# Projecting queries and keys without padding, in a four-block sequence model whose attention alternates with other matmuls

## The chip, the cores and the metric

The kernel runs on one core of a Trainium2 chip. Everything is 32-bit floating point. The metric is the time of one execution on the device in microseconds (us). The engines are TensorE (PE, with its weight load PEld), VectorE (DVE), ScalarE (ACT), GpSimd (POOL) and SyncE (SP, which here only issues transfers). All runs of the kernel before: 2048.16, 2049.68 and 2059.28 us, median 2049.68.

## The reference

Four blocks act on x, which has 4 sequences of 512 tokens with 288 features, under one condition vector for each sequence.

```python
def attention(h):                      # blocks 0, 1 and 3; 16 heads of 18
    q, k, v = split(h @ w_qkv + b_qkv)     # block 3: no biases here
    p = softmax(q @ k.T * 18 ** -0.5)      # 512 x 512 for each head and sequence
    return (p @ v) @ w_proj + b_proj

# blocks 0, 1, 3: six vectors from the condition shift, scale and gate
x = x + gate1 * attention(layernorm(x) * (1 + scale1) + shift1)
h = layernorm(x) * (1 + scale2) + shift2
x = x + gate2 * feed(h)
# feed, block 0: top 2 of 4 experts (288 -> 1152 -> 288, gelu by tanh)
# feed, blocks 1 and 3: one MLP of the same size (gelu by tanh; exact gelu)

# block 2: U from QR of a 288 x 64 matrix, R = expm(skew matrix of the condition)
x = x + (x @ U @ R - x @ U) @ U.T
```

## The kernel before

**Stages.** L0's attention, the experts, L1's attention and MLP, the rotation of block 2, L3's attention and MLP follow one another. The QR and the matrix exponential of block 2 are done in small portions beside other stages.

**Rounds.** An attention has 16 rounds, `groups[r]`: batch b = r // 4, group g = r % 4 of four heads. A head has 18 features, padded to 32 partitions, so that a group fills the 128 partitions of a tile (`qks[r, 0]` for queries, `qks[r, 1]` for keys, three buffers each, shifting through rounds). The score work is in quads of four matmuls with 32 rows each, which run side by side in PE's four row groups: two from `row_max` (queries against keys; DVE takes the maximum of each row straight from the bank) and two from `weight` (keys against queries of an earlier round, one round and one quad behind; ScalarE takes the exponential from the bank). `shift` ends a round: four transposes bring the row maxima into a bank, and DVE subtracts them from the queries, in a nineteenth row of each head, against which the keys hold a one. Thus the second product has the maximum subtracted already. A round has eight quads; after quads 1 and 5 come `sums`, the products of the exponentials with the values.

**Gaps.** After each quad other work is put in by a dictionary `pieces` from gap number to a string, one letter for each piece: Q is `queries_and_keys` of the next round, X is values (`values`) or output projection (`project`), A transposes the next batch's activations, R is routing for the experts. The order of PE is fixed as written: `mm` (line 76) ties each matmul to the one before it, so every matmul has line 76 in the profile. `take`, `beside_of` and `in_turn` fix the order of other engines in the same way, without a wait. `work_off` takes pieces; at the round's end what remains of each job is drained.

**Banks.** PSUM has eight banks (line 64): four with the tag "sc" for the tiles of the quads, three with the tag "de" for everything else (`misc`), and one, `av`, for the sums. A tag's banks are used in turn; a tile waits until its bank's last reader is done.

**Projection.** `queries_and_keys` (lines 829 to 857) multiplies weights that lie padded in DRAM: 8 column chunks of 128, four for queries and four for keys, of which each round takes one and one. The 288 input features are two chunks of 128 and a remainder of 32. ScalarE adds the bias and writes the tile of queries or keys in place (line 856). The bias holds the one of the nineteenth row.

**After the scores.** `collect` sends the raw sums of a round by POOL's queue (`oo<-raw`, 18 x 512 each), and the sums' divisors by SP's queue; `invert` (lines 964 to 974) sends them back inverted. The queue of SP also carries all loads, and in block 0 the copies of expert weights into a table in DRAM (`w1c`).

**Start of block 0.** SP loads x of batch 0, then the attention's weights, and with `load_x` (lines 171 to 173) twelve tiles of x of batches 1 to 3. The first round's projection is made before any score (`first`), and its successors' in the gaps.

**Experts and MLP.** `contraction` (lines 1286 to 1301) multiplies the hidden features by the second weights, into "de" banks; the hidden products use "sc" banks. The rotation (`rotate`, line 1983 on) uses "de" for its small products.

## Time and profile before

The profiled execution took 2033.07 us (its span, from first to last instruction, 2031.4), 16.6 us or 0.8% less than the median of the runs above.

| stage | window, us | PE busy, us | DVE busy, us | ACT busy, us | DMA share |
|---|---|---|---|---|---|
| start | 0 to 48 | 37.28 | 23.51 | 7.51 | 0.73 |
| attention L0, rounds 1 on | 48 to 391 | 334.27 | 243.93 | 167.60 | 0.25 |
| experts | 391 to 931 | 519.08 | 208.71 | 154.07 | 0.59 |
| attention L1 | 931 to 1285 | 342.21 | 269.00 | 168.47 | 0.18 |
| MLP L1 | 1285 to 1470 | 184.19 | 73.72 | 46.52 | 0.17 |
| rotation | 1470 to 1500 | 27.21 | 11.32 | 9.56 | 0.00 |
| attention L3 | 1500 to 1847 | 338.17 | 210.45 | 167.16 | 0.12 |
| MLP L3 | 1847 to 2031 | 174.81 | 33.68 | 44.54 | 0.07 |

The windows are cut at the first and last instructions of a stage as the timeline shows them, to the nearest us. Busy time is the time in which an engine executed something; the DMA share is the mean busy share of 16 DMA engines. A line of the timeline gives the start, the duration, the engine, the line, the operation, output and inputs by name (numbers of buffers left out), then shapes, the number of instructions in the row and, in brackets, the idle time before it and what ended it. Durations of matmuls that follow one another overlap, so what one costs is read from the starts.

### The profile page before, as it was taken

To read this page: it belongs to the slowest core of one execution; us is meant where nothing else is said; L and a number is where in the kernel's file an instruction comes from. 1 tells how busy PE (TensorE), PEld (TensorE's weight loads), DVE (VectorE), ACT (ScalarE), POOL (GpSimd) and SP (SyncE) were. 2 spreads that over 40 slices of the span, in tenths; PEclk is the share of its full clock that TensorE was granted. 3 is DMA by queue.
4 is the path that set the end of the run, shared out by engine and by line. 5 is a ranking of instruction groups with operands and counts; after the bars stand their busy time and mean duration, and the time that the engine had idled before them with its cause. 6 is when DMAs were issued, how large, how long until landed. Compare 5 with 4: busy or idle time off the path is not lost.

```text
span 2031.4 us, 29536 instructions
## 1 busy us (share of the span) xinstructions
PE 1957.2 (96%) x10932; PEld 1045.6 (51%) x10932; DVE 1074.3 (53%) x3103; ACT 765.4 (38%) x1409; POOL 569.2 (28%) x803
## 2 busy tenths in 40 slices
PE   7999999999999999999999999999999999999998
PEld 4434444466667777776434443456654344433565
DVE  5666777623454333446777877454255556554211
ACT  1545555333312232322555544421125455555220
POOL 3111221443434446651332122211401111213101
PEclk9989999899999999999999999999999899999999
DMA  7421111447655766751112111220000111111000
GB/s 152 119 52 20 23 33 34 106 121 222 180 155 163 223 191 206 220 183 30 45 42 43 33 39 40 47 69 19 21 1 10 28 29 35 28 27 23 18 16 22
DMA packets 95698, 155.89 MB, mean 77 GB/s; under 512 B 33571, under 2 KB 71310, under 8 KB 95554
## 3 DMA queue, kind: packets, MB, share of 16 engines
q0 software_dynamic: 28672, 89.90, 14.7%
q1 hardware_dynamic: 66770, 64.10, 13.8%
q8 instruction: 86, 1.41, 0.3%
q14 instruction: 58, 0.48, 0.1%
q10 hardware_dynamic: 112, 0.01, 0.0%
HBM read 125.29 MB, written 18.48 MB: 71 GB/s over the span
## 4 chain that ended last, share of the span: by engine, by line
PE 70%; DVE 7%; DMA 4%; POOL 1%; issue 1%; ACT 1%; SPq 0%; POOLq 0%; DVEq 0%; ACTq 0%
PE e0h L76 9%; PE e0o L76 8%; PE a3m L76 7%; PE a1m L76 6%; PE av L76 6%; PE a3psqk L76 4%; PE f1h L76 4%; PE f3h L76 4%; PE a1psqk L76 4%; PE f1o L76 3%; DVE max L873 3%; PE f3o L76 3%; DMA v<-pT 2%; DMA wr<-in_wrot 1%; PE a3psv L76 1%; PE a3pp L76 1%
## 5 line engine op out<-in xcount | busy, mean ns | idle before, releaser
L873 DVE TENSOR_REDUCE max<-a3m 128x1 f32<-128x512 f32 x256 | 164.6, 686 | 132.9 <-PE a3s L76 122.3
L76 PE MATMUL e0h<-e0hT,e0w 128*128 128x256 f32 (+1 forms) x1188 | 229.0, 404 | 4.9 <-DMA e0w<-w1c,wrow 4.2
L873 DVE TENSOR_REDUCE max<-a0m 128x1 f32<-128x512 f32 x256 | 165.3, 683 | 94.3 <-PE a0s L76 81.7
L873 DVE TENSOR_REDUCE max<-a1m 128x1 f32<-128x512 f32 x256 | 165.8, 684 | 75.0 <-PE a1s L76 68.4
L76 PE MATMUL e0o<-e0w,e0hm 128*128 128x288 f32 x756 | 201.6, 417 | 0.0
L76 PEld LDWEIGHTS e0h<-e0hT,e0w 128*128 128x128 f32 (+1 forms) x1188 | 166.2, 189 | 62.3 <-issue 37.1
L885 ACT ACTIVATE a0p<-a0s 128x512 f32<-128x512 f32 x256 | 140.2, 596 | 146.8 <-PE a0s L76 146.7
L885 ACT ACTIVATE a1p<-a1s 128x512 f32<-128x512 f32 x256 | 140.9, 596 | 142.4 <-PE a1s L76 142.1
L885 ACT ACTIVATE a3p<-a3s 128x512 f32<-128x512 f32 x256 | 140.0, 596 | 139.2 <-PE a3s L76 139.1
L76 PE MATMUL a1m<-a1qk,a1qk 32*128 32x512 f32 x512 | 159.2, 647 | 8.0 <-DVE max L873 6.9
L76 PE MATMUL a0m<-a0qk,a0qk 32*128 32x512 f32 x512 | 159.4, 647 | 6.4 <-DVE max L873 5.3
L76 PEld LDWEIGHTS e0o<-e0w,e0hm 128*128 128x128 f32 x756 | 141.9, 192 | 42.5 <-issue 4.0
L76 PE MATMUL a0s<-a0qk,a0qk 32*128 32x512 f32 x512 | 160.4, 655 | 1.3 <-DVE max L873 1.3
L76 PE MATMUL a1s<-a1qk,a1qk 32*128 32x512 f32 x512 | 159.8, 647 | 0.2 <-DVE u L547 0.2
L76 PE MATMUL a3m<-a3qk,a3qk 32*128 32x512 f32 x512 | 152.1, 647 | 6.8 <-DVE max L873 5.5
L76 PE MATMUL a3s<-a3qk,a3qk 32*128 32x512 f32 x512 | 153.5, 647 | 0.3 <-DVE a3qk L927 0.3
L1279 ACT ACTIVATE e0hm<-e0h,e0w 128x256 f32<-128x256 f32 x189 | 89.5, 473 | 166.7 <-PE e0h L76 166.7
L607 POOL TENSOR_TENSOR nrm<-n,phalf 64x1 f32<-64x1 f32 (+31 forms) x64 | 36.6, 573 | 297.9 <-DVE n L604 294.1
L1813 ACT COPY e0r<-e0o 128x288 f32<-128x288 f32 x44 | 17.5, 398 | 184.1 <-PE e0o L76 176.4
L76 PEld LDWEIGHTS a1m<-a1qk,a1qk 32*128 32x128 f32 x512 | 47.4, 184 | 72.8 <-DVE max L873 44.1
L76 PEld LDWEIGHTS a0m<-a0qk,a0qk 32*128 32x128 f32 x512 | 47.4, 185 | 67.9 <-DVE max L873 38.8
L76 PE MATMUL f1h<-f1hT,w 128*128 128x512 f32 (+1 forms) x216 | 80.8, 614 | 0.4 <-ACT f1hT L502 0.4
(465 smaller groups left out, 3270.0 us busy)
## 6 DMA issues: line engine op xcount, KB each, us to landing
eo<-e0r SPq DMA_DIRECT2D x44, 144.0 KB
ada<-in_ada SPq DMA_DIRECT2D x18, 324.0 KB
wr<-in_wrot SPq DMA_DIRECT2D x16, 288.0 KB
g<-gates SPq DMA_DIRECT2D x24, 144.0 KB
w1c<-in_w SPq DMA_DIRECT2D x20, 144.0 KB
w<-in_w SPq DMA_DIRECT2D x6, 432.0 KB
x<-in_x SPq DMA_DIRECT2D x16, 144.0 KB
w1c<-in_w SPq DMA_DIRECT2D x8, 288.0 KB
```

Of the source, the lines that this page charges most:

```text
L76: ins = nc.tensor.matmul(*args, **kwargs).ins
L607: in_turn("POOL", nc.gpsimd.tensor_tensor(nrm, n2, phalf[0:n], ALU.pow))
L873: take("DVE", nc.vector.tensor_reduce(m[:, t, i, D : D + 1], ps, AX.X, ALU.max))
L885: take("ACT", nc.scalar.activation(p, ps, AF.Exp, scale=D**-0.5))
L1279: nc.scalar.activation(self.hms[i][f], ps[r][:, 0 : self.width], func, bias=b1(f)),
L1813: take("ACT", nc.scalar.copy(y, ps))
```

## The change

- The padded weights of queries and keys become 576 columns without padding, in five chunks of 126 columns (7 heads of 18; the last has 72). `queries_and_keys` computes one chunk in a round, two in the round before a new batch. A chunk is two remainder matmuls and four products of 256 tokens, in two "de" banks; ScalarE adds the bias into a tile `u`.
- `heads_of` sends each head's 18 rows of `u` into the padded tiles: four transfers for queries on SP's queue, issued in the round's first Q piece, from a chunk that was computed a round earlier (except in the first round and for a new batch), and four for keys issued by ScalarE, two after the chunk's last product and two in later Q pieces.
- The padding of the three sets of query and key tiles is written once (`padding`); `row_max` uses 18 rows, and `shift` multiplies the queries with a mask and subtracts the maxima in one DVE instruction.
- Banks: five "sc" and two "de". Contraction and rotation take "sc"; side work inside an attention takes "sc" (`aside_bank`).
- The strings of pieces are set anew. In odd rounds an X job that still has pieces at the round's end is left to the next round (`left`), where they are W in gap 0. A quad's order is scores, maximum, scores, maximum.
- Start of block 0: the padded weights are loaded into x's room of batches 1 to 3 (`wide`), ScalarE copies them to the compact tiles (`narrow`), then x of these batches is loaded in three transfers of 576 KB on SP's queue (`load_whole`); biases come by 11 transfers on POOL's queue. For L1 and L3 twelve transfers from DRAM to DRAM compact the weights during L0's attention (`compacting`), in runs of 72 bytes.
- The values of the first two token tiles are computed before the first scores. The routing pieces of rounds 11 to 14 move to other gaps.

```diff
-    banks = {"sc": 4, "de": 3}
+    banks = {"sc": 5, "de": 2}
...
+    def load_whole(b):
+        to = x[:, b * NT : (b + 1) * NT, :]
+        nc.sync.dma_start(to, a["x"][b].rearrange("(t p) c -> p t c", p=P))
...
+        def step(l, k, n):
+            to = compact[l][n, :, k, :]
+            src = a[f"wqk{l}"][:, k, n * NG * P : (n + 1) * NG * P]
+            src = src.rearrange("p (h e) -> p h e", e=DP)[:, :, 0:D]
+            beside_of("SP", nc.sync.dma_start(to, src))
...
             def queries_and_keys(r):
 
-                yield
                 b, g = groups[r]
...
+                early = g > 0
+                for c in range(g + 1 if g else 0, g + 2):
+                    yield
+                    if early:
+                        heads_of(r, 0)
+                    m = min(UC, 2 * C - c * UC)
+                    cols = slice(c * UC, c * UC + m)
+                    ps = [bank("de", f"{name}psqk{r}_{c}_{k}") for k in range(2)]
...
+                    for k in range(2):
+                        product(k, MC, slice(k * RR, (k + 1) * RR))
+                    u = us[b, c] = pool.tile([P, T], F32, tag="u", name=f"{name}u{r}_{c}")
+                    for k in range(2):
+                        for n in range(MC):
                             yield
...
+                            product(k, n, slice(0, P))
+                        nc.scalar.activation(
...
+                    if c == 0:
+                        heads_of(r, 0)
+
+                for i in range(GH):
+                    heads_of(r, 1, [i])
+                    if i > 0:
+                        yield
+
+            def heads_of(r, s, which=range(GH)):
+
+                b, g = groups[r]
+                for i in which:
+                    c, row = divmod((2 * g + s) * GH + i, HC)
+                    o, u = qks[r, s][i * DP : i * DP + D, :], us[b, c]
+                    if s == 0:
+                        in_turn("SP", nc.sync.dma_start(o, u[row * D : (row + 1) * D, :]))
+                    else:
+                        beside_of("ACT", nc.scalar.dma_start(o, u[row * D : (row + 1) * D, :]))
...
-                take("DVE", nc.vector.tensor_sub(q, q, ps))
+                take(
+                    "DVE",
+                    nc.vector.scalar_tensor_tensor(q, q, mask, ps, ALU.mult, ALU.subtract),
+                )
...
-                pieces = {0: "QQ", 2: "QQQ", 3: "QQQ", 4: "XQX", 6: "XX", 7: "X"}
+
+                pieces = {0: "WWQ", 2: "QQ", 3: "QQ", 4: "QXX", 5: "Q", 6: "XX", 7: "X"}
+                if g == NG - 1:
+                    pieces = {0: "QQQ", 2: "QQ", 3: "QQQ", 4: "QQ", 5: "Q", 6: "QXX", 7: "X"}
...
+                if r in left:
+                    jobs["W"] = left.pop(r)
...
-                    pieces = {0: "QQA", 2: "QQQ", 3: "QQQ", 4: "QAA", 6: "XXX", 7: "XX"}
+                    pieces = {0: "QQQ", 2: "QQ", 3: "QAA", 4: "QA", 6: "XX", 7: "X"}
...
-                    quad([(row_max, r, k)] + lagging(8 * r + k - 9))
+                    quad(lagging(8 * r + k - 9) + [(row_max, r, k)])
...
+                        if r % 2 and r < n - 1 and "X" in jobs:
+                            left[r + 1] = jobs.pop("X")
...
-                ps = bank("de", f"{self.name}o{i}_{t}")
+                ps = bank("sc", f"{self.name}o{i}_{t}")
...
-    load_x(1)
-    load_x(2)
-    load_x(3)
+    w["narrow"]()
+    for b in range(1, B):
+        load_whole(b)
```

## The prediction

> **What bounds the kernel now.** I read the page's busy row and clock row first. TensorE (PE) is the bound, at its full clock nearly throughout.
>
> ```profile
> PE 1957.2 (96%) x10932; PEld 1045.6 (51%) x10932; DVE 1074.3 (53%) x3103; ACT 765.4 (38%) x1409; POOL 569.2 (28%) x803
> PEclk9989999899999999999999999999999899999999
> ```
>
> Then the table by stage, for the rounds of the attentions of L0, L1 and L3 (columns: window, length, busy time of PE, weight load, DVE, ACT and POOL, granted clock, DMA share, GB/s). PE idles 9 to 12 us in each stage of 16 rounds, 0.5 to 0.75 us a round.
>
> ```profile
> 48.00:391.00 343.00, 334.27 (x2065) 143.72 (x2062) 243.93 (x608) 167.60 (x298) 71.11 (x113) 0.98 0.25 57
> 931.00:1285.00 354.00, 342.21 (x2032) 145.60 (x2030) 269.00 (x667) 168.47 (x295) 85.43 (x130) 0.99 0.18 39
> 1500.00:1847.00 347.00, 338.17 (x2027) 144.23 (x2026) 210.45 (x391) 167.16 (x294) 58.16 (x97) 0.98 0.12 24
> ```
>
> Last the timelines of PE, DVE and ACT inside a round of L3: they show what a gap between two quads costs when it has too little work.
>
> ```profile
> 1700.20 1.03 PE L76 MATMUL a3psqk<-a3hT,wqkr 32*128 32x512 f32 x4
> 1708.77 1.56 PE L76 MATMUL a3psqk<-a3hT,wqk 128*128 128x256 f32 x6
> 1710.27 0.69 PE L76 MATMUL a3m<-a3qk,a3qk 32*128 32x512 f32 x1
> ...
> 1563.20 1.24 PE L76 MATMUL a3psv<-wv,a3hT 128*128 128x288 f32 x4
> 1564.37 0.69 PE L76 MATMUL a3m<-a3qk,a3qk 32*128 32x512 f32 x1
> 1564.63 0.69 PE L76 MATMUL a3m<-a3qk,a3qk 32*128 32x512 f32 x1
> 1565.68 0.75 PE L76 MATMUL a3psv<-wv,a3hT 128*128 128x288 f32 x2
> 1566.27 0.92 PE L76 MATMUL a3sh<-ident,max 128*128 128x128 f32 x4
> 1567.13 0.69 PE L76 MATMUL a3m<-a3qk,a3qk 32*128 32x512 f32 x1
> ```
> ```profile
> 1563.29 1.29 DVE L873 TENSOR_REDUCE max<-a3m 128x1 f32<-128x512 f32 x2 [1.62 <-PE a3s L76]
> 1564.49 0.45 DVE L827 COPY a3v<-a3psv 128x288 f32<-128x288 f32 x1
> 1567.30 0.69 DVE L927 TENSOR_TENSOR a3qk<-a3qk,a3sh 128x512 f32<-128x512 f32 x1
> ```
> ```profile
> 1563.33 1.09 ACT L885 ACTIVATE a3p<-a3s 128x512 f32<-128x512 f32 x2 [1.83 <-PE a3s L76]
> ```
>
> The quad ends at 1563.20 (T). The pair of row maxima runs T+0.09 to T+1.38, the pair of exponentials T+0.13 to T+1.22. Two tiles of the next quad start at T+1.17, behind the gap's work; the other two need the bank of the second maximum and start at T+1.43. With four score banks, a gap with under 1.43 us of work is stretched to that.
>
> **The change, part by part.**
>
> *Projection.* Prices from L3's rows by their starts: six products of 128x256 take 1.50 us (1708.77 to 1710.27), 0.50 each; the remainder pair of 512 columns 0.96 (1700.20 to 1701.16), so 0.53 for the new pair of 256 columns, by the same rate with 0.05 of start. A batch had 4 x (0.96 + 8 x 0.50) = 19.84; it will have five chunks of 0.53 + 4 x 0.50 = 2.53, 12.65. That is 7.2 us less a batch, 86 us over 12 batches. It is a gain only where the gap it leaves has no floor.
>
> *Five banks.* The fourth tile of a quad then waits for the second exponential (T+1.22), so the floor falls to about T+1.27. An estimate from the rows above.
>
> *A plain round, worked out (L3's sixth).* A quad takes 1.06 (1562.13 to 1563.20), eight 8.5; sums of values 1.85; a product of X or W 0.58; the shift's transposes 0.62. Before, the eight gaps hold 1.46, 1.85, 1.50, 1.50, 1.66, 1.85, 1.17 and 1.20; raising the last two to 1.43 gives 12.7, with the quads 21.2 (measured from shift to shift: 21.17). After, they hold WWQ 1.69, sums 1.85, QQ 1.00, QQ 1.00, QXX 1.17, sums 1.85, XX 1.17, X and shift 1.20; raised to 1.27 that is 11.75, with the quads 20.2. So some 1.0 us of the 2.4 removed here survives the floor, before new waits. The same sum gives 20.1, 20.2, 20.3 and 20.2 for rounds 5 to 8 (measured before: 21.99, 21.17, 21.38, 21.74): 86.3 becomes 80.8.
>
> *New waits on PE in those rounds.* Two spare banks serve projection, values and shift. (i) A round that leaves X pieces has both banks full of values at its end; the shift must wait for DVE's copy (0.45), which stands behind the last quad's maxima (until T+1.38): the shift starts at T+1.83, and with its 0.62 the gap holds 2.45 in place of 1.27. Between 0 (copy done early) and 1.2; I take 1.2, since DVE runs in order. Behind the shift stands the whole next quad. (ii) The next round's Q starts with a bank whose value copy is behind two maxima: between 0 and 1.3; I take 0.7, half way, since two W products run first. (iii) ScalarE issues the keys, two and then one at a time. The only ACT issue in the trace took 0.42 (SP's take 0.4 to 0.7); the exponentials queue behind it, and the score bank behind them: 0 if in its idle time (ACT is 48% busy here), 0.84 if a pair stands in front; I take 0.4 in a plain round, and 0 in the round that projects two chunks, where the issues fall beside the long gap of the sums. In a round that also transposes the next batch, whose evacuations are ACT's too, a half-empty gap (0.53 or 1.00) and these make 0.75.
>
> With these rounds 5 to 8 come to 20.1 + 1.2 + 0.75 = 22.05, 20.2 + 0.7 + 0.4 = 21.3, 20.3 + 1.2 = 21.5 and 21.3: 86.15 against 86.3, nothing gained. Rounds 9 to 12 likewise, +0.6 in all since leftovers follow one another, and rounds 1 and 2 +0.4. Rounds 3, 4 and 13 to 15, with few pieces and no W, fall from 20.5..20.8 to the new floor: -0.7, -0.9, -1.0, -1.0 and -1.8. An attention: -4.4; three: **-13 us**. Bounds: -54 with no new wait (each attention -18: -5.5 for rounds 5 to 8, as much for 9 to 12, -5.4 for light rounds, -2 for rounds 1 and 2); +13 with (iii) at 0.84 in 13 rounds of each (13 x 0.44 x 3 = 17 more) and (ii) at 1.3 in five (5 x 0.6 x 3 = 9 more).
>
> *Start of L0.* Before, the x of batches 1 to 3 and the first scores did not touch:
>
> ```profile
> 28.26 9.03 SPq L173 DMA_DIRECT2D x<-in_x  x12
> 29.91 1.14 PE L76 MATMUL a0m<-a0qk,a0qk 32*128 32x512 f32 x8 [0.78 <-ACT a0qk L856]
> ```
>
> Now the first queries go by DMA on SP's queue, behind three x loads of 576 KB. Twelve loads took 9.03 us of issue at the DMA rate of this stretch; the queries need the data before them out of the way, then about 2 us (a 36 KB transfer SBUF to SBUF, `oo<-raw`, takes 1.9 to 2.1 to landing). First scores at 38 to 40: **+9 us**, between +3 (only key and query latency) and +13. The six narrowing copies on ACT run while the first activations are still awaited. POOL's eleven bias transfers stand before its later issues, all due tens of us later; cover gone, 11 x 0.5.
>
> *Starts of L1 and L3*: query and key DMAs in front of the first scores, 2 us, less the values moved under them: **+1.5 each, +3** (0 to 5).
>
> *Experts and rotation in the score banks.* Their outputs share the ring with the hidden products; about ten direct neighbours wait 0.4 more for a ScalarE copy (0.40 a copy): **+4** (-4, if five banks relieve it, to +10).
>
> *DVE's side work* (reflections, gates) in L0 and L1, where DVE is busy 244 and 269 us instead of 210, lengthens (i) and (ii), since the copies now gate a shared bank: **+4** (0 to +15).
>
> *Clock.* In round 4 of L0 and L3 the clock was halved for some 10 us and the round took 25.4 instead of about 20.9; the same sums row shows it.
>
> ```profile
> 1594.79 3.40 PE L76 MATMUL av<-a3p,a3v 128*19 128x512 f32 x16
> 1713.91 1.91 PE L76 MATMUL av<-a3p,a3v 128*19 128x512 f32 x16
> ```
>
> It befell rounds whose gaps are nearly empty; the change makes most rounds more like that. I take one more, **+5** (-9 if both go, +27 if six join). [...]
>
> *Compaction and the rest.* Twelve transfers of 1536 runs stand on SP's queue in L0's rounds; the nearest, 384 runs, took 0.84 to 2.3 us, so 3.4 to 9.2. What stands behind them are queries wanted a round (21 us) later and divisors wanted later still: 0, or up to +9 if one query is late each time by 0.8. The shift's subtraction becomes a three-operand form on DVE beside 0.69: 0 to +0.3 a round on the chain, counted in (i). Scores before maxima in the quad: 0, four run at once. Query transfers wait on SP for ScalarE's projection tile; behind them stand divisors and loads with rounds to spare: 0, or 9 if L0's expert loads, which fill its DMA slices, start each round 0.6 later.
>
> **Sum.** -13 + 9 + 3 + 4 + 4 + 5 = +12 us on the profiled execution's 2033.07, 2045. That execution is 16.6 us (0.8%) below the median of the runs, 2049.68; the same ratio gives **2062**. A measurement of this kernel can tell about 0.5%, 10 us, from no change.
>
> **Rivals.** *A, faster*: the waits (i) to (iii) hide, because copies slip in ahead of the maxima and key issues fall into ACT's idle half. Then -54 + 25 = -29, 2020; with the other costs at their low ends (3 + 0 - 4 + 0 - 9 = -10), 1985. For it: 86 us of work really go from an engine at 96%. Against it: DVE's order in the row at 1564.49, the copy after both maxima. It decides where less than half of the waits remains. *B, no change*: half of the waits, -33 + 25 = -8, 2041 to 2053. *C, much slower* on one mechanism: the half clock in four to ten more rounds at 4.5 us, so 2080 to 2107. For it: round 4 lost it in two attentions of three; against it: L3's last three rounds, as light, kept it.
>
> **How the numbers follow.** My forecast, slower by 0.5 to 1.5%: 0.34. C: 0.13. B: 0.19. A: 0.34. The likeliest's own range, by its bounds, is 2052 to 2080; what of it is under 2060 is counted with B. A and C both hold much, so the range runs from A's middle to C's upper part, 2000 to 2100. Faster 0.34, same 0.19, slower 0.47.
>
> **What would show it.** PE's busy time down by 80 to 90 us, and its idle time up by as much. In a plain round, the shift's first transpose more than 1 us behind the last value product, waiting for DVE's value copy; Q's remainder at gap 0 waiting for the same; exponentials behind ACT's issues. First scores of L0 at 38 us or later, released by a DMA. The half clock in more than three rounds. I am wrong if full rounds fall below 20.5 us, if the shift is not held, or if L0's scores start before 33.

## The result, and the profile after

The changed kernel takes 2166.28 us (2165.46 to 2170.8) against 2053.02 for the kernel before on the same chip: 1.055 times, 95% interval 1.052 to 1.059. The forecast was 2062, range 2000 to 2100: 0.6% slower was expected, 5.5% was measured.

The page of the changed kernel, busy row and clock row:

```profile
PE 2018.7 (93%) x10692; PEld 1058.6 (49%) x10692; DVE 1080.8 (50%) x3123; ACT 752.6 (35%) x1439; POOL 573.9 (27%) x814
PEclk9878999899996999999989899899998999999999
```

TensorE has 240 matmuls fewer and yet is busy 61 us longer than in the profile of before, where the prediction expected 80 to 90 us less; its idle time rose by 72 us, near what was expected. The longer busy time goes with a lower clock. The profile gives a mean granted clock of 0.936 against 0.983. Adding up the clock in steps of 1 us, as the window view gives it, there are 277 us at half clock (68 in the profile of before), in 33 stretches that last multiples of 3.4 us, but for the last, which the run's end shortens.

A second profile of the kernel before (2052.07 us) was taken with the experiments. It shows how far the stages vary when nothing is changed, and is the better base, since its total lies nearer the median. Stages from the first instruction of one to the first of the next, with the half clock in each:

| stage, us / half clock, us | before | before, second profile | changed |
|---|---|---|---|
| start | 30 / 0 | 29 / 0 | 34 / 0 |
| attention L0 | 380 / 24 | 376 / 17 | 410 / 85 |
| experts | 527 / 17 | 558 / 55 | 578 / 72 |
| attention L1 | 362 / 7 | 363 / 10 | 387 / 65 |
| MLP L1 | 171 / 0 | 171 / 0 | 177 / 3 |
| rotation | 38 / 7 | 34 / 0 | 37 / 0 |
| attention L3 | 354 / 10 | 349 / 0 | 370 / 44 |
| MLP L3 | 170 / 3 | 170 / 6 | 172 / 8 |

Against the second profile the span grew by 114 us: 78 in the three attentions, 20 in the experts, 5 at the start, 11 elsewhere. The experts vary by 31 us between two profiles of one kernel, so theirs is the least certain share.

In the timeline of L3 the stall that matters is in round 4. First ScalarE, then SyncE, then TensorE of the changed kernel:

```profile
1703.20 1.09 ACT L989 ACTIVATE a3p<-a3s 128x512 f32<-128x512 f32 x2 [2.02 <-PE a3m L82]
1709.19 0.74 ACTq L961 DMA_DIRECT2D a3qk<-a3u  x1
1709.98 1.57 ACT L989 ACTIVATE a3p<-a3s 128x512 f32<-128x512 f32 x3 [5.69 <-DMA a3or<-a3one]
```
```profile
1701.70 1.59 SPq L1081 DMA_DIRECT2D a3or<-a3one  x2
1703.34 8.33 SPq L193 DMA_DIRECT2D w<-in_w  x8
```
```profile
1706.35 0.33 PE L82 MATMUL a3sh<-ident,max 128*128 128x128 f32 x1 [0.42 <-DVE max L977]
1710.63 1.21 PE L82 MATMUL a3m<-a3qk,a3qk 18*128 18x512 f32 x1 [2.90 <-ACT a3p L989]
```

ScalarE finished its exponentials at 1704.3 and next had to issue one key transfer. It did so only at 1709.19, released by a transfer of SyncE's queue, the inverted divisors `a3or<-a3one`, whose data the keys don't use. The issue took 0.74 us; the wait in front of it took 4.9. Three exponentials, ready long before, stood behind it, and TensorE idled 2.90 us for their banks. L1 has the same in round 8, where ScalarE idled 9.0 us.

The trace's records also show why the issue waits. In this run all 901 transfers of SyncE and all 193 of ScalarE signal their landing on the same eight semaphores (100 and 102 to 108), and the 525 of GpSimd on eight others (111 to 118). This key transfer signals on semaphore 105. So does the transfer of the divisors that was issued at 1701.70: its last signal came at 1709.12, and ScalarE, which waited on 105, issued at 1709.19. Of the six waits of over 1 us in front of a key issue in L1 and L3, four (4.8 to 8.2 us) are of this kind, each behind a SyncE transfer of divisors. The other two, 6.6 us each in the first rounds, ended with VectorE's copy into a tile's padding (L1237). The window view cut at 3.41 us shows what follows (length, busy times of PE, PEld, DVE, ACT and POOL, granted clock, DMA share, GB/s):

```profile
1702.28:1705.70 3.42, 3.42 (x19) 1.48 (x15) 1.98 (x4) 1.09 (x2) 0.00 (x0) 1.00 0.24 20
1705.70:1709.11 3.41, 1.61 (x6) 0.43 (x3) 1.35 (x2) 0.00 (x0) 0.00 (x0) 1.00 0.30 66
1709.11:1712.52 3.41, 1.89 (x8) 1.67 (x10) 0.00 (x0) 1.57 (x3) 0.00 (x0) 0.50 0.50 135
1712.52:1715.94 3.42, 3.42 (x19) 1.78 (x18) 2.44 (x5) 1.24 (x3) 0.00 (x0) 0.50 0.17 48
1715.94:1719.35 3.41, 3.41 (x20) 0.48 (x12) 1.23 (x4) 0.44 (x1) 0.00 (x0) 0.50 0.00 1
1719.35:1722.76 3.41, 3.41 (x21) 1.50 (x21) 1.99 (x5) 2.21 (x5) 2.00 (x4) 1.00 0.17 35
```

One window is half empty, and the next three run at half clock although TensorE is fully busy in two of them. A stall of 2.9 us thus costs about 6: the round takes 26.96 us, against 20.66 for the same round in the second profile of before, itself at full clock. Over the whole changed kernel, of 423 windows of this length at full clock in which TensorE was busy at least 95%, 2 were followed by a window at half clock; of 54 in which it was busy under 75%, 24 were. The other 7 of the 33 stretches follow windows between. The second profile of before has 21 windows under 75%, and half clock follows 9 of them: the odds are much the same there, and the windows fewer.

The windows' length and places are read from the trace's clock records of this run. They hold 0.50 and 1.00 and nothing between, in turn, 33 stretches of each, and each stretch lasts a multiple of 3.413 us, apart from that last one; at half clock it is one to eleven of them.

In L0's early rounds the compaction transfers do the same harm from another side. SyncE's timeline:

```profile
99.60 6.27 SPq L266 DMA_DIRECT2D wqkc<-in_wqk  x2
118.51 6.59 SPq L959 DMA_DIRECT2D a0qk<-a0u  x4
129.81 6.92 SPq L266 DMA_DIRECT2D wqkc<-in_wqk  x3
136.84 7.61 SPq L959 DMA_DIRECT2D a0qk<-a0u  x4
```

Two or three compactions occupy SyncE's issuing for 6 to 7 us. One issue in each of these rows takes most of it (5.59 and 4.36 us); compactions that stand alone take about 0.6. The four query transfers behind them take another 7, but 5.6 to 6.7 also where the compactions are left out (the run with both edits, below). Rounds 2 to 5 of L0 took 28.8, 25.1, 31.4 and 33.1 us (21.5, 20.9, 20.7 and 24.2 in the second profile of before).

The full rounds that ran at full clock are much as the prediction had them. Rounds 5, 6 and 7 of L3 took 21.82, 21.37 and 21.90 (predicted 22.05, 21.3 and 21.5). The ten rounds 5 to 7 and 9 to 15 of L3 add up to 211.9 us, and to 212.2 in the second profile of before: the 17 us of matmul work that these rounds lost (2.4 in each that projects one chunk) are not in the time.

### The profile page after: what moved, and what is told of

Its sections match the earlier page's. It is cut to its first block, busy times and chain, and to the rows that moved or that the text cites. A ratio compares the mean times of both kernels' runs of the same rounds, so it can differ in the third digit from the quotient of the medians.

```text
span 2164.4 us, 30450 instructions
## 1 busy us (share of the span) xinstructions
PE 2018.7 (93%) x10692; PEld 1058.6 (49%) x10692; DVE 1080.8 (50%) x3123; ACT 752.6 (35%) x1439; POOL 573.9 (27%) x814
## 5 line engine op out<-in xcount | busy, mean ns | idle before, releaser
L82 PE MATMUL e0h<-e0hT,e0w 128*128 128x256 f32 (+1 forms) x1188 | 237.7, 414 | 6.3 <-ACT e0hT L1933 1.9
L82 PE MATMUL e0o<-e0w,e0hm 128*128 128x288 f32 x756 | 211.9, 432 | 0.0
L82 PE MATMUL a1m<-a1qk,a1qk 18*128 18x512 f32 x512 | 174.1, 683 | 8.6 <-ACT a1p L989 7.2
L82 PE MATMUL a0m<-a0qk,a0qk 18*128 18x512 f32 x512 | 174.3, 693 | 6.3 <-ACT a0p L989 5.7
L82 PE MATMUL a0s<-a0qk,a0qk 32*128 32x512 f32 x512 | 169.4, 680 | 5.4 <-ACT a0p L989 4.2
L82 PE MATMUL a3m<-a3qk,a3qk 18*128 18x512 f32 x512 | 169.2, 671 | 4.8 <-ACT a3p L989 4.3
L82 PE MATMUL a1s<-a1qk,a1qk 32*128 32x512 f32 x512 | 168.8, 665 | 0.3 <-DVE max L977 0.3
L82 PE MATMUL a3s<-a3qk,a3qk 32*128 32x512 f32 x512 | 163.8, 656 | 0.0
L82 PEld LDWEIGHTS a0s<-a0qk,a0qk 32*128 32x128 f32 x512 | 49.6, 195 | 67.5 <-issue 28.5
L82 PEld LDWEIGHTS a1s<-a1qk,a1qk 32*128 32x128 f32 x512 | 50.6, 193 | 64.8 <-issue 21.9
```

The source lines that it names most:

```text
L82: ins = nc.tensor.matmul(*args, **kwargs).ins
```

## The experiments

A total is compared with the kernel before on the same chip (its time stands with each), since the medians of that kernel lay between 2037 and 2069 us. Up to the version with all repairs each total is a single run, good to about 10 us (17 runs of the kernel before on one chip spread from 2044.5 to 2063.8), so causes are read from the stages and their half clock.

### What holds ScalarE: keys on another queue

```diff
-                        beside_of("ACT", nc.scalar.dma_start(o, u[row * D : (row + 1) * D, :]))
+                        beside_of("POOL", nc.gpsimd.dma_start(o, u[row * D : (row + 1) * D, :]))
```

> The changed kernel with the key transfers issued by GpSimd's queue instead of ScalarE. Theory of the blocked issuer: in the changed kernel ScalarE's key issue in rounds 4 and 8 waits 5 to 9 us for a transfer of SP's queue (a?or<-a?one), the exponentials behind it come late and TensorE stalls 1.4 to 4.8 us and then loses half its clock for 7 to 17 us. Then TensorE's waits for exponentials at the a?m and a?s tiles (21 us in the three attentions) go, with most of the half clock there (in L0 85 us of half clock, in L1 65, in L3 37): 2085 to 2125 us, the three attentions 40 to 80 us shorter, the experts unchanged at 575 to 580. Theory of the banks: the stalls that cost come from two spare banks, so the attentions keep their half clock and the time stays over 2145. Third theory, light gaps alone make the clock oscillate: over 2145 too, with the exponentials' waits gone.

Measured: 2136.69 (before 2068.67). L1 fell from 387 to 373 us and L3 from 370 to 360, and TensorE's waits for exponentials went from 7.2 to 0.5 us in L1 and from 4.3 to none listed in L3. Rounds 4 and 8, which had the long stalls, fell by 27 us in the two together, and an even full round such as L3's sixth from 21.37 to 20.44. The blocked issuer is shown for L1 and L3, and is worth 22 us there. All three attentions together gained 18, where 40 to 80 were expected: the half clock of the three attentions stayed at 195 us, since other rounds, the first ones above all, had more. L0 did not gain (415), and the total missed the expected band. Its waits show why (engine and tile, releaser, total, times, longest; first TensorE, in L0, then VectorE, in L0 up to 200 us):

```profile
PE a0s L82 <- DVE max L977: 18.5, 4, 10.1
```
```profile
DVE a0den L1075 <- DMA a0den<-a0raw: 22.7, 3, 13.1
```

VectorE is held up in the same way. Its reciprocal of the divisors waits up to 13.1 us for a transfer that stands behind the compactions on SyncE's queue, and the row maxima, for which TensorE waited up to 10.1 us, stand behind the reciprocal. Without the compactions (the run with both edits, below) the longest such wait in these rounds is 2.6 us.

```diff
-                        beside_of("ACT", nc.scalar.dma_start(o, u[row * D : (row + 1) * D, :]))
+                        in_turn("SP", nc.sync.dma_start(o, u[row * D : (row + 1) * D, :]))
```

> The changed kernel with the key transfers on SP's queue, in turn with the queries. Theory of the blocked issuer: ScalarE never stands behind a transfer, but the keys stand behind SP's loads (8.7 us for eight weights of L1's MLP at one place): TensorE waits for keys at the first row maximum of a few rounds instead. 2090 to 2150, between the GpSimd version and the changed kernel. Theory of the banks or of light gaps: over 2145.

Measured: 2235.98 (before 2068.67), slower than any other version and far above what the theory of the issuer gave. L0 took 445 us, and TensorE waited there up to 9.4 us for a transfer of queries or keys (`a0qk<-a0u`), and once 12.5 us for something that the profile doesn't name. On SyncE's queue keys stand behind compactions and loads; that price was underestimated again. How much each of them costs was not tested.

### What the compactions cost: weights laid out before the launch

The projection's weights and biases are put into DRAM unpadded by the code that lays out the inputs; the wide load, the narrowing copies and the twelve compactions go.

```diff
-        first = [biases, lambda: qk(0), lambda: qk(1), qk_rest]
-        if not compact:
-            w["narrow"], w["biases"] = wide(), lambda: biases(nc.gpsimd)
-            first = []
+        first = [qk, qk_rest]
...
-            got = [lambda: features(self.wg[:, :, 0:E], a["wgate"])] + compacting()
+            got = [lambda: features(self.wg[:, :, 0:E], a["wgate"])]
```

> The changed kernel with the weights and biases of the projection laid out unpadded in DRAM before the launch: no wide load and narrowing copies at the start, no twelve DRAM to DRAM transfers of 72-byte runs in L0's rounds, one bias transfer instead of eleven. Theory of the blocked issuer: the key issues of ScalarE in L0's rounds 2 to 5 (28.8, 25.1, 31.4, 33.1 us in the changed kernel, 21.5, 20.7, 25.5, 24.2 before) wait for transfers that stand behind these compactions, so L0's attention falls from 410 to 380 to 392 us, L1 and L3 stay within 5 us, total 2135 to 2150. If the compactions are not what blocks, L0 stays at 405 or more and the total over 2155.

Measured: 2126.75 (before 2039.57). L0 fell to 396, less than expected, with 75 us of half clock left. L3 rose to 381, which was not expected: its half clock went from 44 to 72 us with its code unchanged. So the three attentions are as long as before the edit (1165 and 1166 us), and most of what the total gained is in the experts (548 against 578), which vary by as much. Alone, this run shows the gain in L0 only.

The two together:

> The changed kernel with the key transfers on GpSimd's queue and the weights laid out unpadded before the launch, nothing else. Alone these gave 2136.7 and 2126.8 (against 2166.3), together with the two bank repairs 2058.8. If issuer and compactions are two separate causes: about 2097, and the banks carry the remaining 38. If the bank waits cost little: 2060 to 2075. If the causes overlap: 2105 to 2125.

Measured: 2109.03 (before 2055.59, the median of 17 runs). The attentions are 380, 370 and 358 us, 1108 together; the changed kernel has 1166, either edit alone 1149 and 1165, the kernel before 1088 and 1096. Alone the two edits gave the attentions 18 and 2 us, together 58 of the 78 that they had lost. So the two causes overlap; that a stall left over from one still costs the clock is how I read it. Of the rest, the bank of the shift took 10 us more off the three attentions and the 32 rows 22 (both below, one profile each).

### The banks

```diff
-    banks = {"sc": 5, "de": 2}
+    banks = {"sc": 4, "de": 3}
...
-                ps = bank("sc", f"{self.name}o{i}_{t}")
+                ps = bank("de", f"{self.name}o{i}_{t}")
```

(The rotation's and the side work's banks likewise.)

> The changed kernel with its bank part undone: four score banks and three others, contraction, rotation and side work on the others as before. Theory of the banks: the experts fall from 578 to 525 to 535 us (their activation transposes wait 17.6 us less for ScalarE, and no half clock of 37 us at 658), and the shift's waits for value copies (about 4 of 1.1 us in each attention) go with the half clock of the attentions: at most 2080. Theory of the blocked issuer: the experts fall as said, the attentions keep the stalls behind ScalarE's issues and their half clock: 2105 to 2130. Light gaps alone: as the latter, with gaps stretched to the four-bank floor.

Measured: 2171.69 (before 2068.67), over every band expected: the theory of the banks alone fails. The waits of the shift for value copies were gone and the attentions were no shorter (430, 385, 373). TensorE's waits for exponentials rose instead, in L3 from 4.3 to 12.4 us: with four score banks it feels ScalarE's delays more often. The experts fell to 556, as long as in the second profile of before.

```diff
-                ps = misc(f"{name}sh{r}")
+                ps = bank("sc", f"{name}sh{r}")
...
-                ps = misc(f"{self.name}xt{i}_{c}")
+                ps = bank("sc", f"{self.name}xt{i}_{c}")
```

> The changed kernel with the shift's transposes and the experts' activation transposes in score banks, nothing else; keys still on ScalarE, weights still compacted on the chip. If the banks carry about 38 us: 2115 to 2135, of it 20 to 35 in the experts (578 before the edit), the attentions each 0 to 6 us shorter with their stalls behind ScalarE's issues in place. If less: 2145 or more.

Measured: 2168.44 (before 2055.59). The experts fell to 555, the attentions took 424, 386 and 378. L3's rounds 5 and 7 fell from 21.82 and 21.90 to 20.52 and 20.62, which is wait (i) of the prediction; even rounds rose by 0.5 (the sixth from 21.37 to 21.89). With ScalarE still blocked, stalls and half clock (273 us in the attentions, 195 in the changed kernel) took more than that back. Six versions with two spare banks and the activation transposes on them had experts of 574 to 586, one had 548; with the transposes in score banks 545 to 562. That points to some 20 us for the banks, but it is within the variation of this stage and so not shown.

```diff
-                        if r % 2 and r < n - 1 and "X" in jobs:
+                        if False:
```

> The changed kernel where odd rounds finish their X job in their own last gap instead of leaving pieces. All theories: the shift waits for the second pair's copies and no longer for the first; four odd rounds of each attention grow by about 1.1 us of work, four even ones shrink by as much, the waits at gap 0 go. Theory of the banks: some of the half clock goes, 2130 to 2155. Blocked issuer and light gaps: 2155 to 2170.

Measured: 2162.8 (before 2068.67). Even rounds at full clock fell by about 1 us (L3's sixth 20.43), odd ones stayed (21.83, 21.90): leaving pieces costs an even round 1 us and gives an odd one nothing. The total says nothing beyond its uncertainty.

The ties in the work beside the experts undone, on top of the run with the banks undone:

```diff
-                products([2], turn)
-                gated(done)
+                products([2])
+                gated()
...
-            for _ in range(4):
                 yield
+            yield
             ps = bank("de", f"psr_{first}")
```

> The run with the bank part undone, and besides the order ties in the modulation products and the later use of the rotation weights undone, which run beside the experts. The experts took 527 us before, 578 changed, 557 with the banks undone. If these ties cause the remaining 30 us: 527 to 537. If what remains is the other traffic and the clock: 550 to 560. The attentions as with the banks undone, within 10 us each.

Measured: 2149.06 (before 2039.57), experts 534. Since the unchanged kernel's experts were 527 and 558, this can't be told from chance; the start was 8 us longer than in the run with the banks undone (45 against 37). Inconclusive.

> The kernel before, unchanged, for a second profile. The experts took 527 us in the first profile and 547 and 565 in two kernels that do not touch them. If the 527 is typical: 525 to 535. If the experts vary from run to run with the clock: 540 to 565, and of the 50 us by which the changed kernel's experts were longer, only the part above that is the change's.

Measured: 2052.07, experts 558 with 55 us of half clock. Two edited kernels whose experts are untouched had 547 and 565 (the runs of the kernel before with products left out and with 18 rows, below). So the 527 was the lucky one.

### Work that is not time

Three products of eight in each projection of the kernel before are left out:

```diff
                             yield
+                            if c == 0 and (s, q.start) != (0, 0):
+                                continue
                             mm(
```

> The kernel before with three of the eight products of each projection left out (queries and keys are therefore not the reference's): 1.5 us of TensorE work less in each round, 72 us in all, and nothing else changed. If TensorE's work is the time: 1980 to 1995 against 2050. By the floors of the prediction (a gap is stretched to 1.43 us of four score banks, so QQQ with 1.0 or 0.5 us left in it still takes 1.43): 0.2 us less a round, 2035 to 2050, more only by the clock: if partly empty gaps make the clock halve, 2055 to 2090 with more than 100 us of half clock against 68.

Measured: 2026.66 against 2039.57 on the same chip: 72 us of matmuls are worth 13 by these single runs, and 12 to 19 by the attentions (1077 us, against 1088 and 1096). A full round lost 0.5 us (L3's sixth 20.43, second profile of before 20.93), more than the 0.2 of the floors and a third of the 1.5 removed. It is an estimate of what the removal alone could give with the old banks and gaps. The half clock of the three attentions is 41 us, as in the first profile of before: emptier gaps alone did not make the clock halve more. The 102 us in all lie above the first profile's 68 because of the experts (58 us, 55 in the second profile).

### How many rows the array works on

In the kernel before, the row maxima over 18 rows:

```diff
-                    lhsT=qks[r, 0][heads_rows(i), t * P : (t + 1) * P],
-                    rhs=qks[r, 1][heads_rows(i), :],
+                    lhsT=qks[r, 0][i * DP : i * DP + D, t * P : (t + 1) * P],
+                    rhs=qks[r, 1][i * DP : i * DP + D, :],
```

> The kernel before with one edit: the row maxima's matmuls read 18 rows of a head instead of 32 (rows 19 to 32 of the queries are zero there, so nothing changes in the result). Theory of the rows: the clock follows how much of the array works, so 18 rows in half of the quads' matmuls make windows too light, above all at the starts of the attentions and in light rounds: half clock from 68 us to over 130, time from 2040 to 2050 up to 2075 to 2120. Theory of idle time alone: the matmuls take the same time, so within 10 us of the kernel before, half clock 60 to 90 us.

Measured: 2081.34 against 2063.71. From the second round on, rounds at full clock are unchanged to 0.1 us, but the attentions of L0, L1 and L3 have less of it (window view, the edited kernel, then the second profile of before):

```profile
29.00:412.00 383.00, 375.41 (x2248) 160.40 (x2248) 268.67 (x671) 178.74 (x320) 85.04 (x130) 0.95 0.27 61
976.00:1346.00 370.00, 358.37 (x2098) 149.30 (x2100) 279.30 (x712) 177.21 (x312) 89.89 (x134) 0.97 0.17 38
1552.00:1910.00 358.00, 349.71 (x2101) 145.80 (x2093) 217.37 (x413) 176.36 (x312) 63.80 (x105) 0.97 0.12 24
```
```profile
29.00:405.00 376.00, 366.93 (x2246) 159.00 (x2246) 267.57 (x671) 179.05 (x321) 85.21 (x130) 0.98 0.28 63
963.00:1326.00 363.00, 351.84 (x2098) 147.69 (x2099) 278.91 (x712) 176.93 (x312) 89.52 (x134) 0.99 0.17 38
1531.00:1881.00 350.00, 341.37 (x2101) 144.23 (x2102) 217.36 (x413) 176.86 (x313) 63.77 (x105) 1.00 0.13 25
```

The half clock of the three is 85 us, against 27 and 41 in the two profiles of before, and they are 15 to 23 us longer. It is one run, but its mean granted clock of 0.964 lies outside the range of 43 runs of the unchanged kernel on three chips (0.974 to 0.987). So the same matmuls with fewer rows make the clock halve more often here; at a fixed clock they take the same time.

The other way round, in the changed kernel (a transfer clears the nineteenth row of the queries first):

```diff
-                    lhsT=qks[r, 0][heads_rows(i, D), t * P : (t + 1) * P],
-                    rhs=qks[r, 1][heads_rows(i, D), :],
+                    lhsT=qks[r, 0][heads_rows(i), t * P : (t + 1) * P],
+                    rhs=qks[r, 1][heads_rows(i), :],
...
+                if s == 0:
+                    in_turn("SP", nc.sync.dma_start(qks[r, 0][D::DP, :], zeros))
```

> The changed kernel with row maxima over 32 rows again; one more transfer on SP's queue a round clears the nineteenth rows of the queries before them. Theory of the rows: half clock from 277 us to under 200, 2100 to 2135. Theory of idle time alone: the same time or a little more (one transfer more), 2160 to 2180, half clock 260 to 300.

Measured: 2183.76 (before 2063.71), half clock 285 us: no help. With the long stalls in place the rows made no difference, 195 us of half clock in the attentions with either. This run went against the theory of the rows as a main cause.

### All repairs together

Keys on GpSimd, weights laid out before, shift and activation transposes in score banks:

> The changed kernel with four repairs: keys issued by GpSimd, weights laid out unpadded before the launch, the shift's transposes in a score bank (no wait for value copies), the experts' activation transposes in score banks. Theory of the blocked issuer together with the banks: each attention below its time in the kernel before (380, 362, 354 us) by 0 to 10, the experts at 535 to 555, total 2050 to 2090. If light gaps alone make the clock halve: over 2110, with over 200 us of half clock.

Measured: 2058.81 (before 2039.57); attentions 377, 373 and 347, half clock 188 us.

With 32 rows besides:

> The version with four repairs (2058.8, half clock 188 us) with row maxima over 32 rows and the clearing transfer. Theory of the rows: half clock under 120 us, 2015 to 2035. Theory of idle time alone: 2050 to 2070.

Measured: 2045.61 (before 2063.71); attentions 372, 356 and 347, half clock 139 us. That lies between what the two theories expected. L1 gained 17 us, and kept it in each later profile with 32 rows (354 to 356, against 373); L0 gained 5 and L3 nothing. So the rows count in L1, where no long stall is left.

> As the former, and the ties in the modulation products and the later use of the rotation weights undone, which gave the experts 23 us in the run with the banks undone. Experts from 545 to 525 to 535 us; the rest as in the former. Theory of the rows: 1995 to 2020, less than the kernel before on the same chip. Idle time alone: 2035 to 2055.

Measured: 2055.27 (before 2063.71); experts 558, start 42 instead of 31. Undoing the ties made the start longer and the experts no shorter, so they stay.

The same kernel as the one with 32 rows, in 12 runs:

> The version with all repairs and row maxima over 32 rows, timed against the kernel before. By its first look, 2045.6 against 2063.7 on the same chip, ratio 0.985 to 0.998. The attentions at 372, 356 and 347 us against 380, 362 and 354.

Measured: 2055.49 against 2055.59, ratio 1.000 (0.998 to 1.003): the gain that the single run had promised did not come. The attentions are 378, 356 and 347 us. Its page, and TensorE's longest waits in L3:

```profile
PE 1954.0 (95%) x10692; PEld 1036.6 (51%) x10692; DVE 1082.7 (53%) x3124; ACT 750.4 (37%) x1433; POOL 664.9 (32%) x995
```
```profile
PE a3sh L82 <- DVE max L977: 4.8, 14, 0.4
PE a3pp L82 <- ACT f3hT L578: 1.6, 1, 1.6
```

No wait for an exponential is left, and rounds at full clock take 19.4 to 21.6 us in L3.

> The repaired version again, on the same chip and beside the same runs of the kernel before: ratio 0.995 to 1.005.

Measured: 2047.50 against 2037.37, ratio 1.005 (1.002 to 1.008); attentions 368, 356 and 343.

```diff
+                if t in (1, 2):
+                    fill()
```

(`fill` writes two products of 128x256 into the bank of the sums, which is free in the first round.)

> The repaired version with work added: in the first round of each attention four products of 128x256 that nothing reads, two after the second and two after the third group of scores, 2 us of TensorE work an attention, 6 us in all. There TensorE ran little but matmuls of 32 rows for 3 us before the clock halved (L3: 20.5 us of half clock from 1538, first round 24.6 instead of 20.0 us). If the clock follows the work that the array does in a window: this half clock goes in one to three of the attentions, and the time falls by 2 to 12 us in spite of the added work. If not: up to 6 us longer.

Measured: 2047.47, ratio 1.003 (1.001 to 1.005), in time the same as without. But the half clock went from the place where the work was added. The first round of L1 and of L3, without the fill (the profile of the run above) and with it, in the window view (length, busy times of PE, PEld, DVE, ACT and POOL, granted clock, DMA share, GB/s):

```profile
960.00:977.20 17.20, 16.82 (x57) 8.02 (x57) 16.35 (x45) 0.95 (x2) 5.28 (x8) 0.73 0.25 61
1526.20:1542.10 15.90, 15.52 (x58) 7.50 (x58) 15.14 (x37) 0.95 (x2) 3.69 (x6) 0.79 0.12 33
```
```profile
965.90:980.90 15.00, 15.00 (x66) 8.26 (x66) 14.10 (x40) 0.95 (x2) 4.94 (x8) 1.00 0.26 70
1529.50:1543.60 14.10, 14.10 (x65) 7.96 (x65) 13.27 (x32) 0.95 (x2) 3.69 (x6) 1.00 0.14 37
```

Without the fill a stretch of 10.2 us at half clock began in L1's first round in each of four profiles, and one of 6.8 or 20.5 us in L3's. With it there is none, and these rounds are about 2 us shorter although they hold 2 us more work. L0's first round had no half clock in the run above to save. Elsewhere in this one profile half clock remained, 10 us of it in L3's last round, so the total doesn't show the gain.

So no version timed in repeated runs beat the kernel before. The repaired one equals it. On the chip of the second profile of before, its attentions are 7 us and its experts 3 us shorter, and the start, the rotation with the start of L3, and the MLPs are 10 us longer. Its mean granted clock is 0.962 there against 0.978: what its rounds gain at full clock, half clock takes back.

## Why the prediction was wrong

- **Projection and floors: right for full rounds, wrong for light ones.** The products in L3 went from 256 to 160 matmul rows of the trace as counted (the prediction's "six products" at 0.50 each are three, of two such rows; its sum has this right). Rounds 5 to 7 came out within 0.4 us of the working. That removed work falls into gaps with a floor is shown by the run that only left products out. "Nothing gained" in full rounds holds. But L3's light rounds 3, 13, 14 and 15, at full clock, were to fall by 0.7, 1.0, 1.0 and 1.8, and changed by -0.5, -0.9, -0.3 and +0.6.
- **Round 6 was right by luck.** Its 21.3 held 0.7 for wait (ii) and 0.4 for wait (iii). With the keys on GpSimd it took 20.44, so the issues on ScalarE cost it 0.9 even without a long stall, and at most 0.24 (20.44 less 20.2) is left for wait (ii).
- **Wait (i): right.** It was priced at 1.2, and odd rounds fell by 1.3 when the shift got a score bank. TensorE's waits in L3 of the changed kernel (total, times, longest):

```profile
PE a3sh L82 <- DVE a3v L905: 3.9, 4, 1.1
```

- **Wait (iii): the step that failed.** The working said that ScalarE's issue costs "0 if in its idle time, 0.84 if a pair stands in front", from an issue of 0.42. An issue took 0.74, which would still have done. What was left out is that an issue can wait: for a semaphore on which a transfer of SyncE's queue had yet to signal, 4.9 us in L3's round 4 and 8.2 in L1's round 8, with the exponentials behind it. The trace of before couldn't show this wait, since ScalarE issued only one transfer there, and the bound of 0.84 was no bound. Moving the keys to GpSimd's queue took 22 us off L1 and L3.
- **Compaction: wrong.** The working took 0, "or up to +9", by when the transfers would land. Its cost is in SyncE's issuing, 6 to 7 us where two or three follow one another, and in what VectorE and ScalarE await from that queue. L0 is 34 us longer, and 30 of these went when both the compactions and ScalarE's key issues were removed.
- **Clock: far too small.** Taken as +5, at most +27. Half clock grew by 189 us against the second profile (209 against the first). The sixteen matmuls of a sums row took 3.40 us at half clock and 1.91 at full clock in the profile of before; so at most about half of the time at half clock is lost, up to 95 of the 114 us, including the half clock that the stalls of the previous points brought. Rival C, which named this, had 0.13 and ended at 2107, since it counted light rounds as the only trigger. Lighter gaps alone did not bring it, as the run with products left out shows. What precedes 24 of the 33 stretches is a window in which TensorE was busy under 75%; fewer rows in the row maxima bring more of it too, once the long stalls are gone (188 us with 18 rows, 139 with 32, one profile each). The prediction named half clock in round 4 of L0 and L3; the last rounds of L0 and L1 had some too (3 and 7 us).
- Two spare banks are not shown as the cause of the half clock: with the banks undone it did not fall (318 us against 277), and with the stalls behind transfers removed it did (225).
- **Start of L0:** +9 predicted, +4.4 measured (first scores at 34.27). The DMA share is 0.85 to 1.01 from 24 to 30 us and 0.19 in the two us after, so the x loads seem to have been over by 30 us; the working had them last 9 us.
- **Experts:** +4 predicted, 20 measured against the second profile, -4 to +10 being the bounds given. The activation transposes on two banks were not in the working; that they are the cause is not shown. It took the 527 us of one profile for the stage's time.
- **Starts of L1 and L3, side work of DVE:** +3 and +4 predicted. From the first matmul of the projection to the first score it is 9.1 and 11.4 us, against 5.5 and 5.7 in the second profile, part of it values moved ahead. No run separates these terms.
- The MLP of L1 grew by 6 us; the cause wasn't looked for.

The forecast had the right sign and the wrong mechanism. In the attentions it was slower because ScalarE, and with the keys on GpSimd also VectorE, stood still for transfers (up to 8.2 and 13.1 us at a time), and half clock follows many of these stalls. For most of the other 36 of the 114 us the cause is open.

## What to carry to other kernels

Before moving a transfer's issue to an engine that computes, ask what the issue itself may have to wait for, including transfers of other queues that signal on the same semaphores; its own duration is the small part (here 0.74 us, behind waits of up to 8.2). When TensorE is nearly full, price a stall at itself plus the half clock that may follow. Here it followed 24 of 54 windows of 3.4 us that were busy under 75%, and lasted 3.4 to 17 us in the attentions. A little work put into such a window can cost less than nothing, as the fill showed in two first rounds. And work taken out of a gap was a gain here only down to a floor (0.5 us of the 1.5 taken out of a full round of the kernel before): ask for that floor first.

## What was not expected of the hardware

- In the kernel before, matmuls with fewer rows came with a lower granted clock (0.964 in one run, 0.974 to 0.987 in 43 runs with 32 rows). Eighteen rows instead of 32 in half of the quads' matmuls left rounds at full clock as long, to 0.1 us, and raised the half clock in the attentions from 27 or 41 us to 85.
- Two microseconds of added matmuls in the first round of L1 and of L3 took half clock of 10.2 and 6.8 us or more away, and made these rounds shorter.
- ScalarE's transfers waited for SyncE's, since both signal on the same eight semaphores in the changed kernel (193 and 901 transfers); the longest such wait in L1 and L3 was 8.2 us.
- One kernel's experts took 527 and 558 us in two executions, with 17 and 55 us of half clock.
- Two to three DRAM to DRAM transfers in runs of 72 bytes held SyncE's issuing for 6.3 to 6.9 us, where one alone takes 0.6.
